# Cross-attention with folded weights: two PSUM copies of the last rows of U instead of a PSUM copy and a GpSimd copy, and two pairs' A in one block

## The chip, the cores and the metric

The kernel runs on one core of a Trainium2 chip. The metric is the device time of one execution in microseconds (us), and a time is given as the median of several runs. Five compute and control engines work side by side, each on its own list of instructions in a fixed order: TensorE (PE, matrix products; its weight loads are listed apart as PEld), VectorE (DVE), ScalarE (ACT), GpSimd (POOL), and SyncE (SP), whose queue issues the transfers (DMA) here. Matrix products write to PSUM, eight banks of 128 partitions by 2 KB.

## The reference

Cross-attention with 8 heads of 256 columns, a residual and a layer norm, all in fp32. x is 16 x 256 x 256, the context c is 16 x 77 x 192.

```python
Q = (x @ Wq);  K = (c @ Wk);  V = (c @ Wv)          # each split into H = 8 heads of D = 256
score = einsum('bhqd,bhkd->bhqk', Q, K) / sqrt(256)
score = where(mask, score, -inf)                     # mask: 16 x 77
attn = softmax(score)
out = einsum('bhqk,bhkd->bqhd', attn, V) @ Wo + x    # heads laid side by side before Wo
return (out - mean(out)) * rsqrt(var(out) + 1e-5) * gamma + beta
```

## The kernel before

**What is folded.** Per head h the kernel makes two small weight products once: G_h = Wk_h Wq_h^T / 16 and U_h = Wv_h Wo_h, each 192 x 256. For the context of a group of four batches it makes A_h = G_h^T c^T, so that the scores are x A_h, and for each batch c U_h, which the softmax weights then multiply. The 192 rows are split into the first 128 (tiles gA, uA, cA) and the last 64 (gB, uB, cB).

**Heads in pairs.** Pair a holds the heads 2a and 2a+1, told apart as e = 0 and e = 1. Products of the last 64 rows use only 64 of TensorE's 128 rows, so two of them run side by side, one in the lower and one in the upper half. For that cB holds the same 64 rows of the transposed context in both halves of the partitions, and so does uB: `of_e(uB, e)[half(k), :, a]` is the place of head e of pair a, once in half k = 0 and once in half k = 1.

**PSUM.** All banks come from one ring of eight, `ps_mm`. A new tile takes the bank of the tile eight places before it, and waits until that one has been read.

**The weight stage** (about 6 to 55 us into the span) runs in an order written out by hand; nothing reorders it. With the names as in the code:
- `turn_blk(a)`, L683: VectorE transposes Wk and Wq of pair a (to kT and qT), as blocks of 32.
- `g_of_pair(a)`, L778: TensorE makes the first 128 rows of G (tiles pgb), ScalarE scales them to gA. `rest_of_g_of_pair(a)`, L793: the last 64 rows (phb), which VectorE scales to gB.
- `a_of_pair(a)`, L812: A of the pair for the first group of batches (tiles pa, four banks): `part_A` with gA (L172), `part_B` with gB (L186), then four ScalarE copies to a.
- `turn_v(a)`, L712: VectorE transposes Wv of pair a.
- The loop at L843 makes the first 128 rows of U (tiles pu, two banks for two pairs, one for each e). `evacuate` copies them to uA, by turns on ScalarE and VectorE. For the second two pairs `turn_rest()`, L598, stands ahead of the copies: VectorE transposes the rest of cA and cB, whose transfers land late, and GpSimd makes copies of them (cRA, cB's other half, cRB).
- `bias_of(0, GB)`, L551: two VectorE and three GpSimd instructions that turn the mask into a bias for the scores.
- The loop at L857 makes the last 64 rows of U (tiles pw, L737): the bank of e has pair 2j in its lower half and pair 2j+1 in its upper. ScalarE copies the lower half of each bank to the lower half of uB, VectorE the upper to the upper, and after each GpSimd copies what they wrote to the other half (L865).
- The loop at L866: GpSimd makes a sum of three parts of U, in place zero of uA and uB. Each batch's attention output is computed later with seven products of blocks instead of eight, which needs it.
- `prepare_last()`, L240: products of U with the last 13 keys of every batch, into eight banks (tiles pr): uA of e = 0 (L248), uB of both e (L260), uA of e = 1 (L248).

**After it** a loop over the batches: scores (ps, L289), shift by bias and maximum on VectorE (L304, L311), exponentials on ScalarE (L318), c U of the next batch (pv, L214 and L225), A of the next group (pa), the weighted sums (L422, L354), and the layer norm.

Transfers are issued by SyncE in one order: Wk, Wq and c for the first pair, Wk and Wq of pairs 1 to 3 (L582), Wv (L582), Wo (L626), the rest of c (L593), the mask (L631), x (L140). The second half of Wo goes to the place that held Wq's blocks.

Of the kernel before, what the change touches and what calls it, by code (L numbers as in the profile page):

```python
# [19 lines left out]
GB = 4  # L20
# [5 lines left out]
def kernel(  # L26
# [13 lines left out]
    nc = tc.nc  # L40
# [8 lines left out]
    NF = H // 2  # L49
    KR = S2 - KM  # L50
    BK = 32
# [30 lines left out]
    uB = const.tile([P, 5, NH, NF, BK], F32, tag="uB", name="uB")  # L82
    NS = B - GB - 1

    def of_e(u, e):
        return u[:, 3 - 2 * e : 5 - 2 * e].rearrange("p q n i c -> p (q n) i c")
# [19 lines left out]
    def flat(ap):  # L106
        return ap.rearrange("p a b -> p (a b)")

    def half(i):
        return slice(i * LB, (i + 1) * LB)  # L110

    def load_x(g):
        xg_of[g] = const.tile([P, GT, DI], F32, tag=f"xg{g}", name=f"xg_{g}")
        nc.sync.dma_start(xg_of[g], x_rows[:, g * GT : (g + 1) * GT, :])
# [3 lines left out]
    def evacuate(dst, src):  # L118
        evacs[0] += 1
        if evacs[0] % 2:  # L120
            nc.scalar.copy(dst, src)
        else:
            nc.vector.tensor_copy(dst, src)
# [5 lines left out]
    def in_two(name, shape, g):  # L129
        return pools[g % 2].tile(shape, F32, tag=f"{name}{g % 2}", name=f"{name}_{g}", bufs=1)  # L130
# [22 lines left out]
    def prepare_a(g, places, B_first=False):  # L153


        if 0 in places:
            a_of[g] = in_two("a", [P, 2, GB, H, S2], g)
        parts = [
            (2 * u + i, dc) for u in places for dc in range(2) for i in range(2)
        ]  # L160
        batches = slice(g * GB, (g + 1) * GB)
        banks = []

        def cols(dc, i):
            return slice((2 * i + dc) * BK, (2 * i + dc + 1) * BK)

        def part_A():
            if not B_first:
                banks.extend(ring_of(parts))
            for (h, dc), o in zip(parts, banks):  # L170
                for i in range(NM):
                    nc.tensor.matmul(  # L172
                        flat(o[i * BK : (i + 1) * BK]),
                        gA[:, h, cols(dc, i)],
                        flat(cA[:, batches, :]),
                        start=not B_first,
                        stop=B_first,
                    )

        def part_B():  # L180
            if B_first:
                banks.extend(ring_of(parts))
            for j in range(0, len(parts), 2):
                for i in range(NM):
                    for k, (h, dc) in enumerate(parts[j : j + 2]):
                        nc.tensor.matmul(  # L186
                            flat(banks[j + k][i * BK : (i + 1) * BK]),
                            gB[half(k), h // 2, cols(dc, i)],
                            flat(cB[half(k), batches, :]),
                            start=B_first,  # L190
                            stop=not B_first,
                        )

        def ring_of(parts):
            return [
                ps_mm.tile([P, GB, S2], F32, tag="mm", name=f"pa_{g}_{h}_{dc}") for h, dc in parts
            ]

        def copies():
            return [(a_of[g][:, dc, :, h, :], o) for (h, dc), o in zip(parts, banks)]  # L200

        return part_A, part_B, copies
# [348 lines left out]
    def bias_of(lo, hi):  # L551

        part = bias[:, lo:hi]
        part_f = bias_f[:, lo * S2 : hi * S2]
        nc.vector.tensor_scalar(part_f, part_f.bitcast(I32), 0.0, -MASKED, ALU.is_equal, ALU.mult)
        nan = st.tile([P, hi - lo, 1], F32, tag="nan", name=f"nan_{lo}", bufs=1)
        nc.vector.tensor_reduce(nan[:, :, 0], part, AX.X, ALU.max)
        nc.gpsimd.tensor_tensor(nan, nan, nan, ALU.mult)
        nc.gpsimd.tensor_tensor(nan, nan, nan, ALU.subtract)
        nc.gpsimd.tensor_tensor(part, part, nan.to_broadcast([P, hi - lo, S2]), ALU.add)  # L560
# [3 lines left out]
    with tc.tile_pool(name="wonce", bufs=1) as wp:  # L564
# [118 lines left out]
        def turn_blk(a):  # L683
            for blk, of in ((wk_blk, kT_blk), (wq_blk, qT_blk)):
                nc.vector.transpose(
                    of[a].rearrange("p n (m r) -> p m n r", r=BK),
                    blk[:, a - 1].rearrange("p m (n c) -> p m n c", c=BK),
                )
# [23 lines left out]
        def turn_v(a):  # L712
            nc.vector.transpose(
                wv_turned[:, a].rearrange("p n (m r) -> p m n r", r=BK),
                wvT[:, a].rearrange("p m (c n) -> p m n c", n=4),
            )
# [29 lines left out]
        def two_banks(name, j):  # L746
            return [ps_mm.tile([P, 2, DI], F32, tag="mm", name=f"{name}_{j}_{e}") for e in range(2)]
# [30 lines left out]
        def g_of_pair(a):  # L778

            banks = [ps_mm.tile([P, DI], F32, tag="mm", name=f"pgb_{a}_{e}") for e in range(2)]  # L780
            for n in range(4):
                for e in range(2):
                    nc.tensor.matmul(
                        banks[e],
                        kT_blk[a][half(e), n, :P],
                        qT_blk[a][half(e), n],
                        start=(n == 0),
                        stop=(n == 3),
                    )
            for e, o in enumerate(banks):  # L790
                nc.scalar.mul(gA[:, 2 * a + e], o, D ** -0.5)

        def rest_of_g_of_pair(a):  # L793

            banks = [ps_mm.tile([P, P], F32, tag="mm", name=f"phb_{a}_{e}") for e in range(2)]
            for n in range(4):
                for i in range(2):
                    for e in range(2):
                        nc.tensor.matmul(
                            banks[e][half(i)],  # L800
                            kT_blk[a][half(e), n, P:],
                            qT_blk[a][half(e), n, i * P : (i + 1) * P],
                            start=(n == 0),
                            stop=(n == 3),
                        )
            for e, o in enumerate(banks):
                for i in range(2):
                    nc.vector.tensor_scalar(
                        gB[half(e), a, i * P : (i + 1) * P], o[half(i)], D ** -0.5, None, ALU.mult
                    )  # L810

        def a_of_pair(a):  # L812
            part_A, part_B, copies = prepare_a(0, (a,))
            part_A()
            part_B()
            for dst, src in copies():
                nc.scalar.copy(dst, src)
# [7 lines left out]
        turn_c()  # L825
        rest_of_g()
        turn_blk(1)
        a_of_pair(0)
        for a in range(1, NF):
            g_of_pair(a)  # L830
            rest_of_g_of_pair(a)
            if a + 1 < NF:
                turn_blk(a + 1)
            else:
                for i in range(3):
                    turn_v(i)
            a_of_pair(a)
        load_x(0)
        nc.sync.dma_start(gam, gamma.partition_broadcast(P))
        nc.sync.dma_start(bet, beta.partition_broadcast(P))  # L840
# [2 lines left out]
        for j in range(NF // 2):  # L843
            pu = two_banks("pu", j)
            for a in range(2 * j, 2 * j + 2):
                of_pair(pu, a, wv_part, wo_part)
            if j:
                turn_rest()
            for e in range(2):
                evacuate(  # L850
                    of_e(uA, e)[:, :, 2 * j : 2 * j + 2].rearrange("p n a c -> p a n c"),
                    pu[e].rearrange("p a (n c) -> p a n c", c=BK),
                )


        bias_of(0, GB)
        for j in range(NF // 2):  # L857
            for e, pw in enumerate(
                rest_of_pairs(j, (2 * j, 2 * j + 1), wv_part, wo_part, "pw")
            ):  # L860
                for i, engine in enumerate((nc.scalar.copy, nc.vector.tensor_copy)):
                    a = 2 * j + i
                    here, there = (of_e(uB, e)[half(k), :, a] for k in (i, 1 - i))
                    engine(here, pw[half(i)].rearrange("p (n c) -> p n c", c=BK))
                    nc.gpsimd.tensor_copy(there, here)  # L865
        for u in (uA, uB):  # L866
            t2, _, b22, b11, b12 = (u[:, q].rearrange("p n i c -> p (n i c)") for q in range(5))
            nc.gpsimd.tensor_tensor(t2, b22, b12, ALU.subtract)
# [16 lines left out]
    for b in range(-1, B - 1):  # L885
# [16 lines left out]
        g, n = (b + 1) // GB + 1, (b + 1) % GB  # L902
# [119 lines left out]
```

## Time and profile before

| | |
|---|---|
| time, median of 5 runs (lowest to highest) | 276.44 us (275.75 to 276.61) |
| the profiled execution's own time | 276.47 us |
| its span in the profile | 274.6 us |
| TensorE busy | 267.7 us (97%) |
| VectorE, GpSimd, ScalarE busy | 210.6, 161.7, 134.1 us |
| GpSimd copies of uB (L865) | 8, 3.57 us from first to last |
| ScalarE and VectorE copies of pw (L864) | 4 and 4, 0.63 us for two and 1.52 us for four |
| ScalarE copies of one pair's pa (L817) | 4, 1.38 us |

All times inside an execution are microseconds from the start of the span, as the profiler recorded one execution. A line of a timeline gives the start, the length, the engine, the line of the code, the operation, what is written from what, the shape and the count; neighbours of one kind are merged. Matrix products are pipelined and their ends are modelled, so a step from start to start says more than a length. "x <- y" in a list of waits says that x waited for y; "issue" is time in which an engine waited for nothing that the profile shows. The chain of waits follows the work that ended last back from the end, at each step to what released it.

### The profile page before, as it was taken

Reading aid. Unit: us, or ns where it says so; the run is one execution under the profiler, and the core shown is the slowest. Engines: PE = TensorE matmul, PEld = TensorE weight load, DVE = VectorE, ACT = ScalarE, POOL = GpSimd, SP = SyncE. Lnnn points to the kernel's source line nnn. Section 1 sums busy time; section 2 is a strip of 40 time slices with the busy share of each in tenths; the row PEclk is TensorE's granted clock in tenths of the full one; section 3 lists DMA queues with packets and bytes.
Section 4 is the critical chain, followed back from the end, with each engine's and each line's share of the span. In section 5 each row is a group of like instructions: output and inputs, shape, how many; then the busy total and the mean of one; then the engine's idle time right before and its main releaser. Section 6 shows DMA issues by size and latency. Waiting matters only on the chain.

```text
span 274.6 us, 13574 instructions
## 1 busy us (share of the span) xinstructions
PE 267.7 (97%) x6056; PEld 188.5 (69%) x6056; DVE 210.6 (77%) x411; ACT 134.1 (49%) x431; POOL 161.7 (59%) x225
## 2 busy tenths in 40 slices
PE   7999999999999999999999999999999999999993
PEld 6655586777494949595958586867777777584662
DVE  0545588379849898979789797878797978889875
ACT  3223312354828283736464646464554644727652
POOL 1000006908887878787868777778787537254754
PEclk9999999999999999999999999999999999999999
DMA  6999989920000232410220405000505060110102
GB/s 190 202 206 187 323 120 191 282 39 2 2 6 2 74 47 60 136 44 4 59 63 24 98 16 182 27 19 11 111 5 117 5 193 2 41 43 4 61 21 76
DMA packets 42458, 22.63 MB, mean 82 GB/s; under 512 B 23632, under 2 KB 41632, under 8 KB 42400
## 3 DMA queue, kind: packets, MB, share of 16 engines
q1 hardware_dynamic: 42400, 21.77, 34.2%
q8 instruction: 47, 0.77, 1.2%
q14 instruction: 11, 0.09, 0.1%
HBM read 17.57 MB, written 4.19 MB: 79 GB/s over the span
## 4 chain that ended last, share of the span: by engine, by line
PE 81%; SPq 9%; DMA 6%; DVE 2%; POOL 1%; issue 1%; DVEq 0%; POOLq 0%
PE ps L289 24%; PE pv L214 10%; PE pa L172 9%; PE po L422 9%; PE pm L422 8%; PE po L354 7%; PE pv L225 6%; PE pa L186 5%; SPq L593 4%; SPq L582 3%; DMA wk_blk<-in_L_xattn_Wk_dram 3%; DMA wvT<-in_L_xattn_Wv_dram 2%; PE pr L260 1%; PE pr L248 1%; DMA cB<-in_ctx_dram 1%
## 5 line engine op out<-in xcount | busy, mean ns | idle before, releaser
L318 ACT ACTIVATE e<-s,top 128x77 f32<-128x77 f32 x256 | 67.0, 346 | 69.1 <-DVE top L311 68.9
L332 POOL TENSOR_TENSOR p<-e,rden 128x512 f32<-128x512 f32 x64 | 47.6, 764 | 43.7 <-DVE rden L326 28.4
L289 PE MATMUL ps<-a,xT 128*32 128x154 f32 x2048 | 70.0, 294 | 0.0
L289 PEld LDWEIGHTS ps<-a,xT 128*32 128x32 f32 x2048 | 66.0, 110 | 1.9 <-issue 0.8
L304 DVE TENSOR_TENSOR s<-ps,bias 128x308 f32<-128x308 f32 x64 | 30.1, 475 | 18.1 <-PE ps L289 18.1
L172 PE MATMUL pa<-cA,gA 128*32 128x308 f32 x512 | 36.2, 423 | 0.0
L214 PE MATMUL pv<-uA,cA 128*32 128x512 f32 x256 | 30.4, 592 | 0.0
L455 POOL TENSOR_TENSOR xg<-xg,m 128x256 f32<-128x256 f32 x33 | 24.1, 730 | 10.5 <-DVE xg L469 8.8
L172 PEld LDWEIGHTS pa<-cA,gA 128*32 128x32 f32 x512 | 16.2, 110 | 20.5 <-issue 8.1
L324 DVE TENSOR_REDUCE den<-e 128x8 f32<-128x616 f32 x32 | 24.8, 776 | 4.4 <-ACT e L318 4.4
L311 DVE TENSOR_REDUCE top<-s 128x8 f32<-128x616 f32 x32 | 25.4, 795 | 1.1
L342 DVE STREAM_TRANSPOSE pT<-p 128x640 f32<-128x640 f32 x32 | 25.3, 813 | 0.8 <-POOL p L332 0.8
L923 ACT COPY vw<-pv 128x512 f32<-128x512 f32 x32 | 17.1, 585 | 8.1 <-PE pv L225 8.1
L385 POOL TENSOR_TENSOR ts<-vw 128x768 f32<-128x768 f32 x11 | 20.2, 1840 | 0.0
L538 DVE SCALAR_TENSOR_TENSOR xg<-xg,rstd,bet 128x256 f32<-128x256 f32 x24 | 18.8, 783 | 1.8
L186 PE MATMUL pa<-cB,gB 64*32 64x308 f32 x512 | 20.0, 420 | 0.0
L600 POOL COPY cRA<-cA 128x208 f32<-128x208 f32 x1 | 0.4, 356 | 29.2 <-DVE cA L599 29.2
L186 PEld LDWEIGHTS pa<-cB,gB 64*32 64x32 f32 x512 | 9.4, 107 | 11.9 <-issue 8.6
L225 PE MATMUL pv<-uB,cB 64*32 64x512 f32 x256 | 17.4, 601 | 0.0
L354 PE MATMUL po<-vw,pT 128*32 128x256 f32 x288 | 17.3, 380 | 0.0
L923 ACT COPY a<-pa 128x308 f32<-128x308 f32 x48 | 16.8, 458 | 0.0
L469 DVE TENSOR_TENSOR xg<-po,xg 128x256 f32<-128x256 f32 x31 | 11.7, 414 | 5.2 <-PE po L422 4.6
(118 smaller groups left out, 402.0 us busy)
## 6 DMA issues: line engine op xcount, KB each, us to landing
xT<-in_x_dram SPq DMA_DIRECT2D x32, 128.0 KB, 4.5
xg<-in_x_dram SPq DMA_DIRECT2D x4, 1024.0 KB, 6.5
out_dram<-xg SPq DMA_DIRECT2D x11, 256.0 KB, 2.6
wo<-in_L_xattn_Wo_dram SPq DMA_DIRECT2D x4, 512.0 KB, 6.5
wq_blk<-in_L_xattn_Wq_dram SPq DMA_DIRECT2D x12, 128.0 KB, 4.4
wvT<-in_L_xattn_Wv_dram SPq DMA_DIRECT2D x16, 96.0 KB, 4.1
out_dram<-xg SPq DMA_DIRECT2D x10, 128.0 KB, 1.7
wk_blk<-in_L_xattn_Wk_dram SPq DMA_DIRECT2D x12, 96.0 KB, 4.5
```

The source lines that it names most:

```text
L172: nc.tensor.matmul(flat(o[i * BK : (i + 1) * BK]), gA[:, h, cols(dc, i)], flat(cA[:, batches, :]), start=not B_first, stop=B_first,)
L186: nc.tensor.matmul(flat(banks[j + k][i * BK : (i + 1) * BK]), gB[half(k), h // 2, cols(dc, i)], flat(cB[half(k), batches, :]), start=B_fir ...
L214: nc.tensor.matmul(pv[k][i * BK : (i + 1) * BK], cA[:, b, k * BK : (k + 1) * BK], uA[:, parts, :, i], start=True, stop=False,)
L225: nc.tensor.matmul(pv[k][i * BK : (i + 1) * BK], cB[half(k), b, k * BK : (k + 1) * BK], uB[half(k), parts, :, i], start=False, stop=True,)
L289: nc.tensor.matmul(ps[m // 2][i * BK : (i + 1) * BK, m % 2 * 2 * S2 : (m % 2 + 1) * 2 * S2], xT_of[g][:, j * NM + m, dc], flat(a_of[g][:, ...
L304: nc.vector.tensor_tensor(s[:, a * H // 2 : (a + 1) * H // 2], ps[a][:, : H // 2 * S2].rearrange("p (h k) -> p h k", k=S2), bias[:, b, :]. ...
L311: nc.vector.tensor_reduce(top, s, AX.X, ALU.max, negate=True)
L318: nc.scalar.activation(e[:, h], s[:, h], AF.Exp, bias=top[:, h : h + 1])
L332: nc.gpsimd.tensor_tensor(part, e_mh[:, :, :, keys], rden_mh.unsqueeze(3).to_broadcast(list(part.shape)), ALU.mult,)
L354: nc.tensor.matmul(po[i * BK : (i + 1) * BK], pT[:, n, i], vw_of[b][:, 2 - n // 2 * 2 : 4 - n // 2 * 2, n % 2, :] if n < NF else vr[:, b, ...
L422: nc.tensor.matmul(out[i * BK : (i + 1) * BK], weight[:, i], moving, start=(n == 0), stop=(n == len(terms) - 1),)
L923: nc.scalar.copy(dst, src)
```

## The change

Three edits, all in the weight stage.
1. uB. The bank of e = 0 is read by ScalarE alone and that of e = 1 by VectorE alone, each twice: once for each half of uB. Every copy comes from PSUM, and GpSimd's copies L865 go. The uA copies no longer take turns by a counter: for the first two pairs e = 0 is ScalarE's and e = 1 VectorE's as before, for the second two both are ScalarE's.
2. A of pair 2 is made together with that of pair 3: G of pair 2, then G of pair 3, then the four `part_A` banks of each pair in one row, then all of `part_B`, then eight ScalarE copies. The transposes of Wk and Wq of pair 3 come ahead of pair 2's gB on VectorE, those of Wv behind pair 3's gB and ahead of A.
3. `bias_of(0, GB)` stands behind the uB copies and ahead of GpSimd's sums of U.

The number and the shapes of the matrix products stay the same, and so does the order on SyncE's queue.

```diff
-        def a_of_pair(a):
-            part_A, part_B, copies = prepare_a(0, (a,))
+        def a_of_pairs(*pairs):
+            part_A, part_B, copies = prepare_a(0, pairs)
             part_A()
             part_B()
             for dst, src in copies():
                 nc.scalar.copy(dst, src)
...
         turn_blk(1)
-        a_of_pair(0)
+        a_of_pairs(0)
         for a in range(1, NF):
             g_of_pair(a)
+            if a == 2:
+                turn_blk(3)
             rest_of_g_of_pair(a)
-            if a + 1 < NF:
-                turn_blk(a + 1)
-            else:
-                for i in range(3):
-                    turn_v(i)
-            a_of_pair(a)
+            if a == 1:
+                turn_blk(2)
+                a_of_pairs(1)
+        for i in range(3):
+            turn_v(i)
+        a_of_pairs(2, 3)
...
-            for e in range(2):
-                evacuate(
+            for e, copy in enumerate((nc.scalar.copy, nc.scalar.copy if j else nc.vector.tensor_copy)):
+                copy(
                     of_e(uA, e)[:, :, 2 * j : 2 * j + 2].rearrange("p n a c -> p a n c"),
                     pu[e].rearrange("p a (n c) -> p a n c", c=BK),
                 )
-
-        bias_of(0, GB)
         for j in range(NF // 2):
             for e, pw in enumerate(
                 rest_of_pairs(j, (2 * j, 2 * j + 1), wv_part, wo_part, "pw")
             ):
-                for i, engine in enumerate((nc.scalar.copy, nc.vector.tensor_copy)):
-                    a = 2 * j + i
-                    here, there = (of_e(uB, e)[half(k), :, a] for k in (i, 1 - i))
-                    engine(here, pw[half(i)].rearrange("p (n c) -> p n c", c=BK))
-                    nc.gpsimd.tensor_copy(there, here)
+                copy = (nc.scalar.copy, nc.vector.tensor_copy)[e]
+                for i in range(2):
+                    for k in range(2):
+                        copy(
+                            of_e(uB, e)[half(k), :, 2 * j + i],
+                            pw[half(i)].rearrange("p (n c) -> p n c", c=BK),
+                        )
+        bias_of(0, GB)
         for u in (uA, uB):
```

## The prediction

> **What bounds the kernel now.** I read the page first. TensorE (PE) is busy for 97% of the span, and its granted clock is nine tenths or more in every slice, so a change pays only where it takes time out of TensorE's own sequence, or puts time into it.
>
> ```profile
> PE 267.7 (97%) x6056; PEld 188.5 (69%) x6056; DVE 210.6 (77%) x411; ACT 134.1 (49%) x431; POOL 161.7 (59%) x225
> PE   7999999999999999999999999999999999999993
> PEclk9999999999999999999999999999999999999999
> ```
>
> The change lies in the weight stage, 14 to 55 us into the span, so the second view is TensorE's timeline there (start, length, line, tile).
>
> ```profile
> 19.76 1.27 PE L186 MATMUL pa<-cB,gB 64*32 64x308 f32 x32
> 21.11 2.00 PE L783 MATMUL pgb<-qT,kT 64*128 64x256 f32 x16
> 23.04 1.10 PE L799 MATMUL phb<-qT,kT 64*64 64x128 f32 x32
> 24.07 2.28 PE L172 MATMUL pa<-cA,gA 128*32 128x308 f32 x32
> 26.28 1.27 PE L186 MATMUL pa<-cB,gB 64*32 64x308 f32 x32
> 27.64 2.00 PE L783 MATMUL pgb<-qT,kT 64*128 64x256 f32 x16
> ...
> 32.81 1.27 PE L186 MATMUL pa<-cB,gB 64*32 64x308 f32 x32
> 34.01 7.18 PE L723 MATMUL pu<-wo,wv_turned 64*128 64x256 f32 x64
> ...
> 47.69 0.57 PE L260 MATMUL pr<-cRB,uB 64*64 64x208 f32 x4
> 48.59 3.03 PE L260 MATMUL pr<-cRB,uB 64*64 64x208 f32 x60 [0.33 <-POOL uB L865]
> 51.55 3.03 PE L248 MATMUL pr<-cRA,uA 128*64 128x208 f32 x32
> ```
>
> Ends are modelled, so I compare starts with starts. The step from pa L186 to the next group is 1.35 us (19.76 to 21.11) and 1.36 (26.28 to 27.64) before a pgb, but 1.20 (32.81 to 34.01) before pu. And pr L260 takes 3.86 us (47.69 to 51.55) with a hole in it. The third view, the list of waits in the same stage, names who is late (total, times, longest).
>
> ```profile
> PEld pgb L783 <- DVE qT L685: 1.3, 2, 0.7
> PEld pr L260 <- POOL uB L865: 1.0, 2, 0.7
> PEld pu L723 <- DVE wv_turned L713: 0.5, 1, 0.5
> PE pr L260 <- POOL uB L865: 0.3, 1, 0.3
> ```
>
> The pu line is no true wait: its 0.5 us is what the weight loads also lose at other changes of tile shape, put down to "issue". The last view is the chain of waits just ahead of the hole.
>
> ```profile
> 45.11 0.71 POOL bias L560
> 45.82 0.05 issue
> 45.87 0.39 POOL uB L865
> ...
> 48.14 0.41 POOL uB L865
> 48.54 0.04 issue
> 48.59 3.03 PE pr L260 x60
> ```
>
> GpSimd (POOL) does the mask's bias first, then eight copies of uB one after the other; TensorE needs the sixth. From 48.59 on the chain is TensorE alone until the last tile.
>
> **Part 1: uB straight from PSUM, bias behind it.** Eight POOL copies (3.57 us in all) go. ScalarE gets 8 copies of 64x256 instead of 4, VectorE 8 instead of 4. The hole: the 60 matmuls after it step 2.96 us, 15 groups of four, so the missing first group adds about 0.19 and L260 without a wait takes 3.15. Saved: 3.86 - 3.15 = 0.71 us. Bounds: at least the 0.33 that TensorE itself sat idle, at most 0.90, if L260 ran its 64 at L248's step of 2.96. I take 0.71, whose row is the same instruction.
>
> Is the new source in time? With part 2's 0.48 us, TensorE starts pr's first part at 44.73 - 0.48 = 44.25, at 2.96 / 8 = 0.37 us a bank; the last two banks, which held pw of pairs 2 and 3, are written from 46.47 and 46.84, and L260 begins at 47.21. ScalarE: the pu copy at 41.21 moves to 40.73, and a second one (0.59, it was VectorE's) ends by 41.95. pw of pairs 0 and 1 was ready for ScalarE at 43.12, so now at 42.64; four copies at 0.63 / 2 = 0.315 end at 43.9. Pairs 2 and 3 are ready at 44.85 - 0.48 = 44.37, and end at 45.63, 0.84 ahead of 46.47. VectorE cannot come before its transpose of cB, which waits for a transfer and ends at 42.73; four copies at 1.52 / 4 = 0.38 end at 44.28, the next four run from 44.37 to 45.9, 0.94 ahead of 46.84. Half of the copies move between partition halves. VectorE's L808 does the same at 64x128 (four in 1.25 us, half of them crossing, 0.28 to 0.29 each), so crossing costs it nothing there. For ScalarE no row crosses; its bounds are 0.315 and, at VectorE's 0.43 us for one whole copy, 0.43, with which it would end at 46.1, still in time. I cost both at nothing.
>
> The Trainium skill, "VectorE: DVE Perf Modes", section "Two Vector instructions with no wait between them", says that an instruction whose first quadrant differs from the previous one's starts only when all earlier ones have finished, which speaks against this order of copies. By that rule the four would not overlap: 4 x 0.43 = 1.7 us, ending at 46.2 instead of 45.9, and the sum would be the same.
>
> What queues behind: bias on VectorE (0.47 each for L555 and L557) now runs at about 46 to 47, its POOL part ends near 48.2. The reader is the shift of the first tile, at 55.91 before, 54.7 now. xT's two transposes (1.30) move from 46.37 to about 47 and end at 48.3; the scores need them at 53.3. The vr memset (0.70) ends at 49.0; vr's copies start after 50.9. On POOL the four U differences (4 x 1.27, and small gaps) end near 53.5 instead of 54.7; their reader pv starts at 58.9 - 1.2. Nothing moves on the DMA queue; the transfers of the mask (39.23, landed 3.8 us later) and of x land before they are asked for.
>
> **Part 2: A of pairs 2 and 3 together.** The matmuls are the same, in another order: G of pair 2, G of pair 3, then 64 of L172 and 64 of L186. Two effects.
> - G of pair 3 no longer waits for qT. VectorE does pair 3's transposes (0.98 + 1.20) right after pair 2's, 21.1 to 23.3; their last transfer (issued at 17.26, 4.2 us) lands at 21.5. TensorE gets there at 24.07. Saved: 1.36 - 1.20 = 0.16 us.
> - Two changes of tile shape fewer. L172 starts a group of four each (2.28 - 0.44) / 7 = 0.263 us, 8 of them 2.10, and the step is 2.21: 0.11 for the change. L186: (1.27 - 0.42) / 7 = 0.121, 0.97 of 1.20: 0.23. Saved: about 0.33, bounds 0 (if each pair pays as now) and 0.33.
>
> Sum 0.49, taken as 0.48: pu starts at 33.53. What could be late there: gA of pair 3 takes ScalarE 0.66 us behind its pgb and is done at 26.8, before the block begins at 27.0; gB of pair 2 now stands behind pair 3's transposes, but these end at 23.3 and its phb is ready only at 24.2. wv_turned now begins after gB of pair 3, near 28.4 instead of 32.00, and four at 1.5 us end at 34.5, each ahead of its reader. wo of pair 0 lands at 32.0 (26.89 + 5.1), the last at 37.3 (28.32 + 9.0) for a need at 38.9. The eight banks of A fill all of PSUM, so pu needs ScalarE's first two copies: these begin 0.84 us after L186 does (19.76 to 20.60 now), so at 32.2, and at 0.345 each end at 32.9, 0.6 us in time.
>
> **Sum.** 0.71 + 0.48 = 1.19 us. The profiled execution took 276.47 us (span 274.6 and 1.87 around it, which I hold); it is 0.03 above the median. 276.47 - 1.19 = 275.28, so 275.3 us. Downstream every step of the chain is TensorE's and starts as much earlier.
>
> **The rivals.**
> - A: part 2 gives nothing, because pu finds its banks still held by ScalarE. Speaks for it: the 0.6 us of cover is thin. Against: ScalarE is idle for 3.3 us ahead of these copies now. Time: 276.47 - 0.71 = 275.8.
> - B: the hole stays and only its owner changes: VectorE or ScalarE hands over pw's banks 0.7 us past the cover. For: 16 copies on two engines that share the stage with transposes. Against: covers of 0.84 and 0.94. Time: 276.47 - 0.48 = 276.0, within what counts as no change (0.2%, 0.55 us, is about what a measurement tells).
> - C, slower: VectorE's eight copies stand behind its transpose of cB, and that behind a transfer issued after a 4.72 us stall of the DMA queue at L593. It lands at 41.5 now; the last copy ends 1.11 + 8 x 0.38 and small gaps later, 4.3 us. Beyond 42.5 TensorE waits, and each further us costs one: landed at 43.7 the whole gain is gone, at 44.7 the time is 277.5. In the old order POOL only needed to follow as well, so a late transfer hurt less. Against: nothing ahead of it on the queue moves.
> - D: the 1.19 us come, but a later stage gives them back, being set by transfers or by VectorE (77% busy). Time 276.4. Against: from 48.59 no step of the chain is anything but TensorE's until 269.9.
>
> **How the numbers follow.** Forecast 0.65, A 0.11, B 0.08, C 0.12, D 0.04. Faster by over 0.2%: the forecast and A, 0.76. Within: B and D, 0.12. Slower: C, 0.12. The forecast's own bounds are gains of 0.16 + 0.33 = 0.49 and 0.49 + 0.90 = 1.39, 276.0 to 275.1. The range adds some 0.3 below for the scatter of the runs shown (275.75 to 276.61) and 0.1 above: 274.8 to 276.1, which holds the forecast, A and B.
>
> **What would show it.** Right: no POOL L865 rows; pr L260 as one run of 64 with a step near 3.15 and no wait; pgb of pair 3 starting 1.04 us after phb of pair 2; one run of 64 for L172 and for L186, pu near 33.5; ps of the first tile near 53.3 instead of 54.51; the loop's steps as before (4.19 for ps). Wrong: a wait of pu on ScalarE's a, of pr L248 or L260 on VectorE or ScalarE uB, or a new wait inside the loop.

## The result, and the profile after

| | before | changed |
|---|---|---|
| median | 276.44 us (55 runs, 275.46 to 278.76) | 274.99 us (29 runs, 274.20 to 276.29) |
| ratio | | 0.9951, 95% interval 0.9940 to 0.9962 |
| profiled execution, its span | 276.47, 274.6 us | 274.95, 273.2 us |
| first pgb of pair 1 | 14.59 us | 14.14 us |
| first ps | 54.51 us | 53.04 us |

The change is 1.45 us faster (by the interval 1.05 to 1.66). The forecast was 275.3 us, 0.3 above, and 274.99 lies in the range. The two spans differ by 1.4 us, and all of it is there when the first scores start (54.51 - 53.04 = 1.47): what follows takes 220.1 us in one (274.6 - 54.5) and 220.2 in the other.

TensorE's timeline of the changed kernel in the weight stage (start, length, line, tile):

```profile
19.31 1.27 PE L186 MATMUL pa<-cB,gB 64*32 64x308 f32 x32
20.67 2.00 PE L783 MATMUL pgb<-qT,kT 64*128 64x256 f32 x16
22.59 1.10 PE L799 MATMUL phb<-qT,kT 64*64 64x128 f32 x32
23.70 2.00 PE L783 MATMUL pgb<-qT,kT 64*128 64x256 f32 x16
25.63 1.10 PE L799 MATMUL phb<-qT,kT 64*64 64x128 f32 x32
26.66 4.35 PE L172 MATMUL pa<-cA,gA 128*32 128x308 f32 x64
30.95 2.30 PE L186 MATMUL pa<-cB,gB 64*32 64x308 f32 x64
33.18 7.18 PE L723 MATMUL pu<-wo,wv_turned 64*128 64x256 f32 x64
40.29 3.68 PE L737 MATMUL pw<-wo,wv_turned 64*64 64x256 f32 x64
43.91 3.27 PE L248 MATMUL pr<-cRA,uA 128*64 128x208 f32 x32
47.10 3.04 PE L260 MATMUL pr<-cRB,uB 64*64 64x208 f32 x64
50.08 3.03 PE L248 MATMUL pr<-cRA,uA 128*64 128x208 f32 x32
53.04 3.22 PE L289 MATMUL ps<-a,xT 128*32 128x154 f32 x92
```

L260 is one run of 64 with a step of 2.98 us (47.10 to 50.08), where it was 3.86. From the second pgb to pu it takes 12.51 us (20.67 to 33.18), where it was 12.90. But L248 ahead of L260 now steps 3.19 (43.91 to 47.10) instead of 2.96: a new wait of 0.23. Its owner is in VectorE's timeline of the same kernel:

```profile
41.82 1.11 DVE L601 STREAM_TRANSPOSE cB<-cB 64x896 f32<-64x896 f32 x1 [0.52 <-DMA cB<-in_ctx_dram]
42.96 3.49 DVE L864 COPY uB<-pw 64x256 f32<-64x256 f32 x8
46.48 0.32 DVE L555 TENSOR_SCALAR bias<-bias 128x308 f32<-128x308 int32 x1
```

The eight copies end at 46.45, and pr's last bank, asked for at 43.91 + 7 x 0.37 = 46.50, gets its release just too late: it starts at 46.60, 0.15 after the copies. The chain of waits of the changed kernel has its last break in the stage there:

```profile
43.98 2.61 PE pr L248 x28
46.59 0.01 issue
46.60 0.57 PE pr L248 x4
47.17 2.98 PE pr L260 x64
```

The profile puts this break down to "issue" and names nobody. That VectorE is the owner is read from the 0.15 us: the same 0.15 lies between copies and product in the run with the bias ahead (below), where the profile does name VectorE.

So the stage from the first pgb to the first ps is 1.02 us shorter (39.92 to 38.90), and the other 0.45 us is that TensorE came to the stage earlier, ahead of any changed instruction. Whether that 0.45 belongs to the change was the first question for the experiments.

### The profile page after: what moved, and what is told of

It is laid out like the page before. It is cut to its first block, busy times and chain, and to the rows that moved or that the text cites. A ratio compares the mean times of both kernels' runs of the same rounds, so it can differ in the third digit from the quotient of the medians.

```text
span 273.2 us, 13577 instructions
## 1 busy us (share of the span) xinstructions
PE 266.5 (98%) x6056; PEld 188.6 (69%) x6056; DVE 211.7 (78%) x414; ACT 136.1 (50%) x436; POOL 158.5 (58%) x217
## 3 DMA queue, kind: packets, MB, share of 16 engines
HBM read 17.57 MB, written 4.19 MB: 80 GB/s over the span
## 4 chain that ended last, share of the span: by engine, by line
PE 91%; DMA 5%; SPq 2%; DVE 1%; issue 0%; DVEq 0%
PE ps L289 25%; PE pa L172 11%; PE pv L214 10%; PE po L422 9%; PE pm L422 8%; PE po L354 7%; PE pv L225 6%; PE pa L186 5%; DMA wk_blk<-in_L_xattn_Wk_dram 5%; PE pu L723 3%; PE pr L248 2%; PE pgb L783 1%; PE pw L737 1%; PE pr L260 1%; PE po L370 1%; SPq L582 1%
## 5 line engine op out<-in xcount | busy, mean ns | idle before, releaser
L172 PE MATMUL pa<-cA,gA 128*32 128x308 f32 x512 | 36.0, 423 | 0.0
L172 PEld LDWEIGHTS pa<-cA,gA 128*32 128x32 f32 x512 | 16.3, 110 | 20.6 <-issue 7.9
L186 PE MATMUL pa<-cB,gB 64*32 64x308 f32 x512 | 19.8, 420 | 0.0
L186 PEld LDWEIGHTS pa<-cB,gB 64*32 64x32 f32 x512 | 9.5, 107 | 11.6 <-issue 8.1
```

The source lines that it names most:

```text
L172: nc.tensor.matmul(flat(o[i * BK : (i + 1) * BK]), gA[:, h, cols(dc, i)], flat(cA[:, batches, :]), start=not B_first, stop=B_first,)
L186: nc.tensor.matmul(flat(banks[j + k][i * BK : (i + 1) * BK]), gB[half(k), h // 2, cols(dc, i)], flat(cB[half(k), batches, :]), start=B_fir ...
```

## The experiments

Each stage length below is from the first pgb of pair 1 to the first ps of one profiled execution; times are medians, and the ratios are against the kernel before on the same chip. That kernel's own median moved between sets of runs (276.34 us beside the first four experiments, 276.83 beside the next four), so medians of different sets are compared by their ratios. A median is set beside one profile with care: in thirteen of the fourteen profiles the execution took 221.9 to 222.3 us beyond its first ps (before, 276.47 - 54.51 = 221.96), so the first ps tells that one execution's time, not the median.

**The change taken apart.** Four kernels, each with a part of the change.

Edits 1 and 3 without A together (against the changed kernel):

```diff
-            if a == 2:
-                turn_blk(3)
             rest_of_g_of_pair(a)
-            if a == 1:
-                turn_blk(2)
-                a_of_pairs(1)
-        for i in range(3):
-            turn_v(i)
-        a_of_pairs(2, 3)
+            if a + 1 < NF:
+                turn_blk(a + 1)
+            else:
+                for i in range(3):
+                    turn_v(i)
+            a_of_pair(a)
```

> Edits 1 and 3 without edit 2: uB twice from PSUM, bias behind it, A pair by pair as before. The measure is the stage from the first pgb of pair 1 to the first ps, 39.92 us before and 38.90 after, which leaves out the head, where the two profiles differ by 0.45 us with nothing changed. Theory (the two parts add up, the hole ahead of L260 is worth about 0.65 to 0.88 us, and VectorE's late copies only cost where A is early): stage 39.05 to 39.25, no wait of pr on uB, time about 0.8 us below before. Rival (VectorE's copies hold pr's last bank here too): stage 39.4 or more, with a step of pr L248 above 2.96.

275.19 us, ratio 0.9955 (0.9938 to 0.9971). Stage 39.04, first ps at 53.06, L248 steps 2.97, L260 2.97. The theory's expectation for the stage, but 1.15 us off the time instead of 0.8.

A together alone: the same lines the other way round, against the kernel before.

> Edit 2 alone: A of pairs 2 and 3 together, uB and bias as before. Theory: the steps from the second pgb to pu shrink by 0.39 us as in the whole change, but the copies of uB on GpSimd follow a transfer of the context that lands at a fixed time, so L260's hole grows by nearly as much: its sixth copy still ends near 48.5. Stage 39.8 to 39.95, time within 0.2 us of before. Rival (the parts add up): stage 39.5, time 0.4 us below before.

276.37 us against 276.34, ratio 0.9994 (0.9977 to 1.0010): nothing that can be told, as expected. TensorE's timeline in this kernel shows where the gain goes:

```profile
33.45 7.18 PE L723 MATMUL pu<-wo,wv_turned 64*128 64x256 f32 x64
47.14 0.57 PE L260 MATMUL pr<-cRB,uB 64*64 64x208 f32 x4
48.38 3.03 PE L260 MATMUL pr<-cRB,uB 64*64 64x208 f32 x60 [0.67 <-POOL uB L867]
```

pu starts at 33.45 instead of 34.01 (0.23 of this is an earlier first pgb, 14.36), and the 60 products of L260 at 48.38 instead of 48.59: the step of L260 has grown from 3.86 to 4.20. GpSimd's copies keep their own time, because they follow a transfer, through VectorE's transpose of cB. That transpose before, and then in this kernel:

```profile
41.62 1.11 DVE L601 STREAM_TRANSPOSE cB<-cB 64x896 f32<-64x896 f32 x1 [1.00 <-DMA cB<-in_ctx_dram]
```

```profile
41.41 1.11 DVE L601 STREAM_TRANSPOSE cB<-cB 64x896 f32<-64x896 f32 x1 [0.34 <-DMA cB<-in_ctx_dram]
```

The first ps comes 12.89 us after its start in both (54.51 and 54.30): it moved by 0.21 us with the transpose, and not by the 0.56 that TensorE was ahead at pu.

The bias alone moved behind the uB loop (against the kernel before):

```diff
-        bias_of(0, GB)
         for j in range(NF // 2):
...
+        bias_of(0, GB)
         for u in (uA, uB):
```

> Edit 3 alone: bias_of moved behind the uB loop, uB still copied by GpSimd from uB. Theory A (what held GpSimd was the bias ahead of its copies, and ScalarE and VectorE write their halves in time): the copies run from about 44.3 to 47.9, the sixth ends at 47.0 ahead of 47.7, the hole goes, stage 39.05 to 39.25. Theory B (the eight copies themselves are too slow, so the copies straight from PSUM were needed): the hole stays above 0.5 us, stage 39.6 or more.

275.45 us, ratio 0.9964 (0.9950 to 0.9978): 0.89 us, more than half of the gain, although the stage in the profile shrank only to 39.60 and L260 still steps 3.53, a little over 0.5 us of waiting. In this execution the context landed late, and GpSimd followed it, as its timeline shows:

```profile
43.64 0.93 POOL L602 COPY cB<-cB 64x896 f32<-64x896 f32 x1 [1.06 <-DVE cB L601]
44.63 0.35 POOL L603 COPY cRB<-cB 128x208 f32<-128x208 f32 x1
45.05 3.58 POOL L864 COPY uB<-uB 64x256 f32<-64x256 f32 x8
```

VectorE's transpose of cB started at 42.41 here, 41.62 in the profile before. By the stage theory B holds, by the time theory A nearly does. The distance from the transfer decides more: the first ps came 11.28 us after the start of cB's transpose (53.69 - 42.41), where it was 12.89. So moving the bias took 1.61 us out of the path behind the transfer, and what hole is left comes with a transfer that was 0.79 later.

The copies of edit 1 with the bias left ahead of them (against the kernel with edits 1 and 3):

```diff
+        bias_of(0, GB)
         for j in range(NF // 2):
...
-        bias_of(0, GB)
         for u in (uA, uB):
```

> The copies of edit 1 with the bias left ahead of the uB loop, A as before. Theory A (once GpSimd's copies are gone the bias only delays VectorE's copies by 0.95 us, and they end at about 47.2 with pr's last bank needed at 47.3): hole gone, stage 39.05 to 39.35. Theory B (the bias must move too): VectorE is late by 0.5 us or more, stage 39.6 or more, with a wait of pr L248 for VectorE's copies.

276.10 us, ratio 0.9988 (0.9969 to 1.0007): no gain that can be told. Theory B: the hole only moves to L248, which steps 3.56 us (44.77 to 48.33), and its owner is VectorE now, whose last copy ended at 47.68, 0.15 ahead of the product that waited. VectorE's timeline in this kernel, and then TensorE's:

```profile
43.08 0.69 DVE L555 TENSOR_SCALAR bias<-bias 128x308 f32<-128x308 int32 x1 [0.54 <-DMA bias<-in_mask_BxS_if_dram]
43.81 0.47 DVE L557 TENSOR_REDUCE nan<-bias 128x4 f32<-128x308 f32 x1
44.20 3.48 DVE L863 COPY uB<-pw 64x256 f32<-64x256 f32 x8
```

```profile
47.83 0.57 PE L248 MATMUL pr<-cRA,uA 128*64 128x208 f32 x4 [0.38 <-DVE uB L863]
48.33 3.04 PE L260 MATMUL pr<-cRB,uB 64*64 64x208 f32 x64
```

My expectation had left out that the bias instruction itself waits for the mask's transfer, 0.54 us.

**Is edit 1 needed at all?** On one chip, with the changed kernel again beside three others. First the changed kernel itself:

> The changed kernel unaltered, to stand beside the next three on one chip. Theory so far (before the change the end of the weight stage is set by the context's last transfer and what queues behind it; after it, by TensorE's own chain from the head): first ps between 52.9 and 53.3 us, time 275.0, some 1.4 us below before. If the gain is only the stage's 1.02 us, 275.4.

275.12 us (6 runs, 274.77 to 275.48; the kernel before 276.83), ratio 0.9945 (0.9923 to 0.9966), first ps at 52.97, as expected. The median lies nearer to 275.0 than to 275.4, but the interval (a gain of 0.94 to 2.13 us) does not tell these two apart. This second profile of the changed kernel has no wait on VectorE:

```profile
44.06 3.03 PE L248 MATMUL pr<-cRA,uA 128*64 128x208 f32 x32
47.03 3.04 PE L260 MATMUL pr<-cRB,uB 64*64 64x208 f32 x64
```

Both step 2.97 (L260 to 50.00). The copies ended 0.12 earlier than in the first profile, at 46.33, and TensorE came 0.24 later (first pgb at 14.38), so the stage is 38.59 with nothing left to wait for.

Edits 2 and 3 without edit 1, so with GpSimd's copies:

> Edits 2 and 3 without edit 1: GpSimd still copies uB, with the bias behind it, and A of pairs 2 and 3 together. Theory (GpSimd's eight copies follow its copies of cB and cRB, so they hang on the transfer): L260 waits for the sixth copy, first ps at 53.4 to 53.8 as with the bias alone (53.69), time 0.4 to 0.8 us below before: A together adds nothing here. Rival (the bias was all that held GpSimd): first ps at 53.1 or less, time as the changed kernel.

274.89 us (6 runs, 274.50 to 275.21), ratio 0.9935 (0.9913 to 0.9957): the same as the changed kernel within the intervals, so the rival holds for the time, though not for its first ps, and my theory falls. GpSimd's copies ran from 44.42 to 48.12, and L260 found them done, with a step of 2.98. GpSimd's timeline in this kernel, and then TensorE's:

```profile
44.42 3.70 POOL L866 COPY uB<-uB 64x256 f32<-64x256 f32 x8
```

```profile
44.39 3.03 PE L248 MATMUL pr<-cRA,uA 128*64 128x208 f32 x32
47.35 3.04 PE L260 MATMUL pr<-cRB,uB 64*64 64x208 f32 x64
```

The first ps came at 53.29 because pair 3's pgb had waited for its qT (a step of 1.63 us after phb, 1.03 without a wait). These 0.60 us also gave GpSimd time: its sixth copy ended near 47.2 (44.42 + 6/8 of 3.70), and without them L260 would have begun at 46.75 and asked for it too early. So this one profile does not show that GpSimd is always in time; that the time is no worse is what the six runs show. The copies straight from PSUM are worth nothing that these runs can show, once the bias is out of the way.

**VectorE's copies.** They took 3.49 us for eight, 0.436 each, where I had 0.38. To see why, each copy was cut in two:

```diff
-                        copy(
-                            of_e(uB, e)[half(k), :, 2 * j + i],
-                            pw[half(i)].rearrange("p (n c) -> p n c", c=BK),
-                        )
+                        for s in (slice(0, 4), slice(4, 8)):
+                            copy(
+                                of_e(uB, e)[half(k), s, 2 * j + i],
+                                pw[half(i)].rearrange("p (n c) -> p n c", c=BK)[:, s],
+                            )
```

> The changed kernel with each copy of pw cut into two of 64x128: of each two, the second starts in the same quarters of the partitions as the first. Theory (a copy that starts in another quarter than the one before waits until that one has ended, as the Trainium skill, VectorE: DVE Perf Modes, section Two Vector instructions with no wait between them, has it): VectorE's starts are unequal, about 0.30 us after a crossing and 0.20 to 0.25 us inside a pair. Rival (reading PSUM for a copy between halves is slower by itself): equal starts of about 0.30 us.

The first starts on VectorE, as the timeline gives them one by one:

```profile
42.19 0.28 DVE L865 COPY uB<-pw 64x128 f32<-64x128 f32 x1
42.40 0.27 DVE L865 COPY uB<-pw 64x128 f32<-64x128 f32 x1
42.68 0.28 DVE L865 COPY uB<-pw 64x128 f32<-64x128 f32 x1
42.89 0.27 DVE L865 COPY uB<-pw 64x128 f32<-64x128 f32 x1
```

Inside a pair the starts are 0.21 us apart, with lengths of 0.28, so they overlap; from one pair to the next, where the half that is read or written changes, it is 0.28 to 0.32 through all sixteen, so the second waits for the first to end. That is the rule that the prediction quoted. One execution, 274.82 us, says nothing on the time.

Then the last of VectorE's copies was given to ScalarE:

```diff
+                        last = 4 * j + 2 * i + k == 7
-                        copy(
+                        (nc.scalar.copy if last else copy)(
```

> The changed kernel, but the last of VectorE's eight copies (the second copy of pw of pair 3, e = 1) is ScalarE's. Theory (VectorE's 0.435 us a copy makes it 0.2 us late for pr's last bank): pr L248 steps 2.96 instead of 3.19, stage 38.7, time 0.2 us below the changed kernel. Rival (the step of 3.19 is a change of tile shape or of banks): step stays 3.19, time the same.

274.96 us (6 runs), ratio 0.9941 (0.9919 to 0.9963), not told apart from 275.12. The experiment failed its purpose: ScalarE's copy waited 0.69 us for VectorE's last one (of the same bank and into the same tile; which of the two held it is not shown), so it ended no earlier, and L248 stepped 3.24. VectorE's timeline in this kernel, and then ScalarE's:

```profile
43.41 3.05 DVE L865 COPY uB<-pw 64x256 f32<-64x256 f32 x7
```

```profile
46.55 0.37 ACT L865 COPY uB<-pw 64x256 f32<-64x256 f32 x1 [0.69 <-DVE uB L865]
```

With that, Wk of pair 2 is transposed ahead of pair 1's gB, and Wq behind it as before; the second argument of turn_blk names which of the two:

```diff
+            if a == 1:
+                turn_blk(2, (0,))
             rest_of_g_of_pair(a)
             if a == 1:
-                turn_blk(2)
+                turn_blk(2, (1,))
                 a_of_pairs(1)
```

> As the run before, and VectorE transposes Wk of pair 2 ahead of pair 1's gB, so that its qT is ready when TensorE asks. Theory: the step of pa L186 of pair 1 goes from 1.36 to 1.20 as its wait for qT goes, stage 38.5, time 0.35 us below the changed kernel. Rival (gB of pair 1 comes late and holds L186, or Wq's transfer has not landed): stage 38.7 or more, no gain over the run before.

Here the step from pa L186 of pair 1 to pgb is 1.19 us instead of 1.36, so that wait is gone; the stage is 38.69, where 38.5 was expected, because pair 3's pgb waited for its qT again (a step of 1.29); the changed kernel beside it had 38.59 without any of this. 274.77 us (6 runs, 274.26 to 275.35), ratio 0.9934 (0.9909 to 0.9959): the lowest median, but its interval overlaps that of the changed kernel beside it, so it is not shown to be faster. The context landed early in this execution (cB's transpose at 40.85), which by itself hides VectorE's lateness.

**Who sets the end of the stage?** If before the change a transfer does, a late TensorE costs nothing; if after it TensorE's own chain does, a late TensorE costs all of it. Four more idle transposes at the head of each kernel:

```diff
-        keep_busy(12)
+        keep_busy(16)
```

> The kernel before with 16 instead of 12 idle transposes at the head, 0.235 us each: TensorE starts up to 0.94 us later, and part of it hides in its first waits for transfers. Theory (before, the context's transfer and GpSimd's copies set the end of the stage): the hole ahead of L260 shrinks by what the head loses, first ps stays within 0.2 us of 54.5, time within 0.25 us of before. Rival (TensorE's chain sets the end in both kernels): first ps and time later by what the first pgb is later.

276.86 us against 276.80, ratio 1.0005 (0.9989 to 1.0020). The first pgb came at 14.82, 0.23 later than before, the step of L260 shrank from 3.86 to 3.40, and the first ps came at 54.28, 0.23 earlier than before: the hole swallowed the late head, and the first ps followed cB's transpose, 12.91 us after its start:

```profile
41.37 1.11 DVE L601 STREAM_TRANSPOSE cB<-cB 64x896 f32<-64x896 f32 x1
```

> The changed kernel with the same four extra transposes. Theory (after the change TensorE's chain sets the end): the first pgb comes 0.3 to 0.9 us later than 14.1 and the first ps by about the same, less the 0.2 us wait on VectorE that it covers; the time moves from 275.0 to 275.2 to 275.7. Rival (a transfer sets the end here too): time unchanged at 275.0.

275.38 us, ratio 0.9952 (0.9934 to 0.9971), but the first pgb came at 14.08: the transposes had hidden in the head's waits for transfers, so this run does not test the question. Its first ps came at 53.06, 11.22 us after the start of cB's transpose (41.84), as in the first profile of the changed kernel (53.04 - 41.82), and with the same wait in L248. Instead TensorE got more work inside the stage:

```diff
-            for a in range(2 * j, 2 * j + 2):
+            for a in (0, 0, 1) if j == 0 else (2, 3):
                 of_pair(pu, a, wv_part, wo_part)
```

> The changed kernel, with U's first 128 rows of pair 0 made twice into the same bank (16 more matrix products, 7.11 / 4 = 1.78 us at L723's step). The extra transposes at the head of the run before hid in waits for transfers (its first pgb came at 14.08), so this adds TensorE work where nothing hides it. Theory (after the change TensorE's chain sets the end of the stage, but for some 0.2 us that VectorE's copies may cost): stage 38.90 + 1.55 to 1.78, first ps near 54.7, time 276.5 to 276.8. Rival (a transfer that lands at a fixed time sets the end here too): time 275.0 to 275.6, and the waits on uB or on the context shrink instead.

276.66 us against 276.72 for the kernel before, ratio 0.9994 (0.9976 to 1.0012): the gain of the change is used up. L723's 80 products step 8.83 us, 1.72 more than the 64; the first ps came at 54.76, 1.72 later than in the changed kernel, and the profiled execution took 276.66, 1.71 more. L248 lost its wait (a step of 2.97). So after the change more work on TensorE is paid in full, but an earlier TensorE gains little: the heads of 14.08 and 14.14 gave a first ps at 53.06 and 53.04, with VectorE's copies behind the transfer last, and the head of 14.38 gave 52.97, with TensorE last. The two chains now end within some 0.3 us of each other: with its head of 14.14 and the stage of 38.59 TensorE alone would have reached the first ps at 52.73.

## Why the prediction was right

The direction, the place and the size held: 275.28 was worked out, 274.99 measured. The gain of 1.19 us lies inside the measured interval (1.05 to 1.66), so the difference from 1.45 is not told from scatter. That it came so close is in part luck: errors in the parts went against each other, and by the stage of the two profiles the gain was 1.02, by the time 1.45. The parts, by its own steps:

- **Part 1, 0.71 us.** The hole is gone. Measured from the start of pr to the end of L260: 6.82 before, 6.17 after, so 0.65. Two errors went against each other. L260 without a wait takes 2.98, not 3.15: the upper bound of the working was the better value. (Sixteen groups in 2.98 are 0.186 each and fifteen 2.79, so by this estimate the step of 2.96 after the wait held some 0.17 that belonged to no group.) And 0.23 was lost in a new wait on VectorE, which I had costed at nothing with a cover of 0.94 us. Of that cover 0.35 went because VectorE's copies ran at 0.436 each from the start, 8 x 0.436 from 42.76 ending at 46.25 instead of 45.9, as the quoted rule of the Trainium skill ("VectorE: DVE Perf Modes", "Two Vector instructions with no wait between them") had said; 0.2 because the context landed later; and 0.34 because TensorE asked earlier (46.50, not 46.84), its head having come 0.45 sooner. The 0.05 that was left did not cover the release, 0.15. In the second profile of the same kernel this wait did not come, so it belongs to the execution as much as to the change. The working had let the rule's 46.2 pass as still covered. The row I took, VectorE's four copies in 1.52, always read and wrote the same halves, and so did not show the case. L808 did show it and was misread: I took its lengths, 0.28 to 0.29, as a sign that crossing is free, but its four starts are 0.31 to 0.32 apart, and each reads another half than the one before, while copies of that shape that keep their halves start 0.21 apart.
- **Part 2, 0.48 us.** The measured step is 0.39. Two changes of tile shape fewer gave 0.13 at L172 (4.29 against 4.42) and 0.33 at L186 with the qT wait (2.23 against 2.56), and 0.08 was lost again: pgb of pair 3 started 1.11 us after phb, not 1.03, because VectorE waited 0.84 for Wq of pair 3, which I had landing at 21.5 and which came near 22.3. This too changes with the execution: in the second profile pgb followed phb by 1.03, in the others with this order by 1.03 to 1.63.
- **The sum, 1.19 us, measured 1.45.** The term that was too small is the hole. In the second profile, where nothing waits, L248 and L260 take 5.94 together instead of 6.82, so the hole was worth 0.88 and not 0.71, and from the second pgb to pu it takes 12.44 instead of 12.90, so part 2 was worth 0.46. Together the stage was 1.33 shorter (39.92 to 38.59). Behind the size lies a step that was mis-sized in kind: I took the hole of the one profile of before as what it costs. Before the change the first ps kept its distance from cB's transpose, 12.89, 12.89 and 12.91 us in the three kernels with the bias ahead of GpSimd's copies, with first pgb at 14.59, 14.36 and 14.82: the chain behind the transfer set it, and TensorE's head only sets how much of it shows as a hole. So the 0.45 us by which the two profiled heads differ are no gain of their own. By these rows the landing and the head of the profile of before would give 1.33 (54.51 less 14.59 + 38.59), and an earlier head at most 1.67 (12.89 less 11.22); the measured 1.45 lies between.
- **The two parts do not add.** A together alone gained nothing that can be told (276.37 against 276.34). Once the bias no longer holds the path behind the transfer, no run tells its gain from nothing either: the ratio is 0.9955 without it, and 0.9951 and 0.9945 with it, and the first ps came at 53.06, and at 53.04 and 52.97. The prediction charged each part by itself; for part 2 that could be right only because part 1 was there too.

**The rivals.** A did not come: the list of waits of the changed kernel names ScalarE's a ahead of pu, but the weight loads lose as much ahead of L186, where nothing is waited for, and pu followed L186 by 2.23 us, near the 2.17 that the working's numbers give (16 x 0.121 + 0.23).

```profile
PEld pa L186 <- issue: 1.0, 2, 0.5
PEld pu L723 <- ACT a L817: 0.5, 1, 0.5
```

B and C came in small, as one thing: 0.23 us of wait on VectorE behind cB's transpose. But C's price was the wrong way round. It held that a late transfer hurt the old order less; over the 0.25 us that these profiles span the old order followed the transfer one for one, 12.89 us behind it, and the new one follows at 11.22, so a late transfer delays both and does not eat the gain. D did not come: every step of the loop is as before (4.19 for ps, 2.19 for pa L172, from start to start).

What the prediction did not see is which edit does the work. It credited the copies from PSUM. The runs show that moving the bias alone brings 0.89 us, that the copies alone bring 0.24 (not told from nothing), that edits 1 and 3 without A are not told from the bias alone (ratios 0.9955 and 0.9964), and that with the bias moved and A together GpSimd's copies do as well (274.89 against 275.12). With the bias out of its way GpSimd was in time in one profile and half a microsecond late in the other. I argued the head of the queue ("does the mask's bias first") and then priced the removal of the copies behind it. Part 1 held both edits under one price, so the sum did not suffer for it; which of them earns the price was not right.

That the run with the bias alone has half a microsecond of hole in its profile and yet 0.89 us in the median is no contradiction. Its profiled execution took 275.64 us, 0.83 less than the 276.47 of before, hole and all, with a transfer 0.79 later. And behind the transfer GpSimd's copies reach the first ps about as soon (11.28 us) as the copies from PSUM do (11.22), which is why edit 1 shows no gain of its own.

What stays open: why the context lands at such different times, and how its landings and TensorE's heads lay in the runs without a profile.

## What to carry to other kernels

A hole behind a chain that starts with a transfer is not a fixed cost: it is the difference between two chains, so read it in more than one execution, and do not add to it the gain of another part that only makes the waiting engine arrive earlier. When an engine's queue is late, ask first what stands ahead in it, and try the reordering alone before moving work to other engines. Price a copy by a row that crosses partitions in the same order; the same shape in the same halves overlaps and looks cheaper.

## What was not expected of the hardware

ScalarE shows the same as VectorE. Before, its two 64x256 copies that keep the same halves started 0.27 us apart at a length of 0.37 (43.12 and 43.39); after, with a half changing each time, they start 0.37 to 0.38 apart (42.30, 42.68, 43.05, 43.43). Cut in two, they start 0.16 apart inside a pair and 0.27 to 0.29 across. And the context's transfers let VectorE start cB's transpose anywhere between 40.85 and 42.41 us in fourteen profiles in which the order on SyncE's queue never changed, a spread larger than the whole gain of this change.
